# A graph-attention and GraphSAGE kernel: the first batch prepared in halves by a written order, block 0's signs read by two engines, the output bias added in parts

## The chip, the cores and the metric

The kernel runs on one core of one Trainium2 chip. The core has TensorE (PE in the profile, PEld for its weight loads), VectorE (DVE), ScalarE (ACT), GpSimd (POOL) and SyncE (SP). SP issues most DMAs; POOL issues some through the software queue. The metric is the device time of a launch in microseconds: the median of the runs, with a profiled execution beside it.

## The reference, cut to what matters

There are 16 batches of 1024 nodes with 128 features. `x` is [16, 1024, 128] in float32, `adj` is a sparse weighted adjacency [16, 1024, 1024] in float32, and `nodemask` is all ones here.

```python
# layer 0: attention
h = relu(layernorm(x))
q, k, v = (h @ W.T + b for each)                 # 8 heads of 16
scores = where(adj == 0, -inf, q k^T / 4)
attn = softmax(scores) * adj
attn = attn / (attn.sum(-1) + 1e-8)
x = x + (attn @ v) @ Wo.T + bo

# layer 1: dilation of the neighbourhoods, then three SAGE layers
h = relu(layernorm(x))
adj_d = adj * keep      # row by row: rank of each neighbour, every sf-th of more than 10 removed,
                        # symmetrically; earlier rows' removals count for later rows
for i in 1..3:
    agg = adj_d @ h / clip(sum(adj_d), 1)
    out = agg @ Wr_i + h @ Wx_i + b_i
    h = batchnorm(relu(out / |out| * mask))      # statistics over all batches and nodes
    h_i = h
x = x + (concat(h_1, h_2, h_3) * mask @ Wl + bl) * mask
```

## The kernel before, in words

The work is one long program in two parts. The order of the instructions of PE, ACT and DVE in the main part is the order in which Python writes them (`manual_schedule`, line 1087). SP's and POOL's instructions, and everything in front of that line, `first_part`'s set-up among it, stand in the order that a scheduler chose.

**Part one** is attention with the dilation beside it. `attention` (line 403) runs over 256 turns (batch b, half c of the query nodes, block m of 128 key nodes), and each turn has two half-turns g, one for each group of four heads. A half-turn on PE adds the mask to the scores (`never` times `nomask`, line 488), adds the products of `qT` and `kT` (line 494), and sums the values of the half-turn before (lines 410 and 415). ACT takes the exponential (two instructions at line 510), and DVE multiplies by the adjacency (two at line 515). So the pair of exponentials marks a half-turn: the text numbers them half-turn 0, 1, 2 and so on. `turn_over` (line 433) prepares a turn two turns ahead: a block of the adjacency is transposed on PE, copied by ACT (line 444), stored to `aT_d`, turned into `nomask` (line 448), and six small DMAs shift `nomask` between partitions (lines 452 and 453). `load` (line 423) brings the block in, three tiles ahead, on SP.

`prepare` (line 254) makes what attention needs of one batch: layer norm (`layer_norm_relu`, line 231; statistics on DVE, the power -1/2 on POOL at line 244, the scaling on ACT at line 250), the transposed activations `hT`, and from them `kT`, `v1` and `qT`. It is a generator, and every `yield` names the place at which the next step may be put. For the batches 1 to 15 its steps are strewn over the half-turns of the batch before. For batch 0 nothing runs yet: lines 461 to 465 turn over two turns and then run all the steps of `prepare(0)` in one go, up to `ready[0]`, before the first score.

`dilation` (line 549) works on 8 blocks of 128 rows of all 16 batches, and `beside_attention` (line 825) puts its steps between the half-turns, paced by the count of half-turns, never by a clock. At its start it reads block 0 of every batch: `fetch(0, b)` (line 573) loads 128 rows by 1024 columns in float32 (512 KB) from `adj` on SP into a tile `ad` with two buffers, and `read(0, b)` (line 579) makes its signs with two ACT instructions that also count the edges. Two batches are read in each of the half-turns 0 to 7. Behind this block the rows of the next blocks are read between other work.

**Part two** is the three SAGE layers L = 0, 1, 2, each with 32 turns (b, c). PE sums over the neighbours (`pg`, line 1011), and for the turn before it DVE and ACT form `o` (line 1029), its squares (line 1034), the square root of their sum (line 1040), the scaled result (line 1044), and PE transposes it (line 1048). In between DVE masks the adjacency of the turn to come (line 139, four pieces). In layer 1, each turn with c = 0 ends with `add_bias` (line 913): ACT multiplies the output bias by the mask of each of the 8 node blocks into `tb`, and DVE adds `tb` to `prev`, the running output.

The tag names the buffer: `mr` has four of 4 KB per partition, which the dilation's working tiles use in part one; `ad` has two; `ps_m` and `ps_d` are PSUM pools of one bank each. `biases` (lines 87 to 100 here, without a function) splits five bias vectors into three bfloat16 pieces, whose rows PE adds by a matmul with ones.

Of the kernel before, what the change touches and what calls it, by code (L numbers as in the profile page):

```python
# [10 lines left out]
F32 = mybir.dt.float32  # L11
BF = mybir.dt.bfloat16
# [9 lines left out]
P = 128  # L22
# [12 lines left out]
def swept(ctx: ExitStack, tc: tile.TileContext, t: dict, out: bass.AP, flag: bass.AP):  # L35
# [52 lines left out]
    n = len(names)  # L88
    bias3 = const.tile([3, n, D], BF, name="bias3")
    with tc.tile_pool(name="setup", bufs=1) as where:  # L90
        vecs = where.tile([1, 2, n, D], F32, name="vecs")
        for i, name in enumerate(names):
            nc.sync.dma_start(vecs[:, 0, i, :], t[name].rearrange("(o d) -> o d", o=1))
        pieces = where.tile([1, 3, n, D], BF, name="pieces")
        for i in range(3):
            nc.vector.tensor_copy(pieces[:, i], vecs[:, i % 2])
            if i < 2:
                nc.vector.tensor_tensor(vecs[:, 1 - i], vecs[:, i], pieces[:, i], ALU.subtract)
        for i in range(3):
            nc.sync.dma_start(bias3[i : i + 1], pieces[:, i])  # L100
# [60 lines left out]
    def first_part(p1):  # L161
# [7 lines left out]
        def load_x(b):  # L169
            if b < B:  # L170
                xts[b] = shared.tile([P, NB, D], F32, name=f"xt_{b}", tag="xin", bufs=3)
                nc.sync.dma_start(xts[b], x[b].rearrange("(k p) d -> p k d", p=P))

        load_x(0)


        nr_i = pool.tile([B * NB, P], I32, name="nr_i", tag="qT")
        nc.sync.dma_start(nr_i, nodemask.rearrange("b (k p) -> (b k) p", p=P))
        nr_f = pool.tile([B * NB, P], F32, name="nr_f", tag="qT")
        nc.vector.tensor_copy(nr_f, nr_i)  # L180
        mps = ps_m.tile([P, 512], F32, name="mps", tag="m")
        nc.tensor.transpose(mps[:, : B * NB], nr_f, ident[: B * NB, : B * NB])
        nc.vector.tensor_copy(mf, mps[:, : B * NB])
        nc.vector.tensor_tensor(mf2, mf, mf, ALU.mult)
        nc.vector.tensor_scalar(
            kill.rearrange("p b k -> p (b k)"), mf, 0.0, -1e5, ALU.is_equal, ALU.mult
        )
# [6 lines left out]
        wps = ps_m.tile([P, 4, D], F32, name="wps", tag="m")  # L194
        for i in range(4):
            nc.tensor.transpose(wps[:, i, :], raw[:, i, :], ident)
        attn_w = one.tile([P, 4, D], F32, name="attn_w")
        nc.vector.tensor_copy(attn_w, wps)
# [13 lines left out]
        nc.vector.tensor_tensor(bq[:, 0:2], own, bq[:, 2:3].to_broadcast([P, 2]), ALU.mult)  # L212
# [3 lines left out]
        for v1 in v1s:  # L216
            nc.gpsimd.memset(v1, 0.0)
            nc.gpsimd.memset(v1[:, :, :, HD : HD + 1], 1.0)
# [5 lines left out]
        zeros = one.tile([P, B * 2 * NB], F32, name="zeros")  # L224
        eps8 = one.tile([P, 32], F32, name="eps8")
# [5 lines left out]
        def layer_norm_relu(dst, src, name):  # L231

            st = shared.tile([P, NB, 6], F32, name=f"st_{name}", tag="lnst", bufs=2)
            mv = shared.tile([P, NB, 2], F32, name=f"mv_{name}", tag="lnmv", bufs=2)
            for i in range(0, NB, 2):
# [4 lines left out]
                if i + 2 < NB:  # L240
                    yield False
            rs = shared.tile([P, 2, NB], F32, name=f"rs_{name}", tag="lnrs", bufs=2)
            nc.vector.tensor_scalar(rs[:, 1, :], mv[:, :, 1], LN_EPS, None, ALU.add)
            nc.gpsimd.tensor_tensor(rs[:, 0, :], rs[:, 1, :], minus_half, ALU.pow)
            yield False
            nc.vector.scalar_tensor_tensor(rs[:, 1, :], mv[:, :, 0], -1.0, rs[:, 0, :], ALU.mult, ALU.mult)
            for i in range(0, NB, 2):
# [6 lines left out]
        def prepare(b):  # L254
# [5 lines left out]
            yield from layer_norm_relu(h, xt, f"a{b}")  # L260
            hT = shared.tile([P, N], F32, name=f"hT_{b}", tag="s", bufs=2)
            for c in range(2):
                yield True
                pt = ps_m.tile([P, 512], F32, name=f"pt_{b}_{c}", tag="m")
# [4 lines left out]

            kT = pool.tile([P, N], F32, name=f"kT_{b}", tag="kT")  # L270
            def query(c):
                pq = ps_m.tile([P, 512], F32, name=f"pq_{b}_{c}", tag="m")
# [7 lines left out]
            def key(c):  # L280
                cc = slice(c * HN, (c + 1) * HN)
                pk = ps_m.tile([P, 512], F32, name=f"pk_{b}_{c}", tag="m")
# [6 lines left out]
            def value(c):  # L289
                pv = ps_m.tile([P, HB, D], F32, name=f"pv_{b}_{c}", tag="m")  # L290
# [11 lines left out]
            for what in (key, value):  # L302
                yield True
                yield from what(0)

            yield "half 1"
            qTs = [pool.tile([P, 2, HN], F32, name=f"qT_{b}_0", tag="qT")]
            yield True
            yield from query(0)
# [93 lines left out]
        def attention():  # L403
# [16 lines left out]
            turns = [(b, c, m) for b in range(B) for c in range(2) for m in range(NB)]  # L420
            tiles = {}

            def load(i):
                if i >= len(turns):
                    return
                b, c, m = turns[i]
                a = pool.tile([P, HB, P], F32, name=f"a_{b}_{c}_{m}", tag="a", bufs=3)
                nc.sync.dma_start(
# [1364 lines left out]
```

## Time and profile before

| | |
|---|---|
| median of 3 runs | 3615.09 us (3610.25 to 3615.42) |
| the profiled execution | 3607.07 us, span 3605.3 us |
| busy in the span | PE 95%, DVE 88%, ACT 64%, POOL 5% |
| first exponential of attention | 36.14 us |
| half-turns 0 to 7, from there to 94.97 us | 58.8 us |
| the 14 half-turns from 95.0 to 153.9 us | 58.9 us |
| layer 1, one turn with c = 0 and the next with c = 1 | 10.48 and 12.71 us |
| layer 2, the same two | 10.47 and 11.67 us |

A profile shows one execution, in microseconds from the span's start. A busy engine need not be the bound; what counts is what ended each wait, and which engine waits for it. A window row gives, for one stretch of time, the busy time and the count of instructions of PE, PEld, DVE, ACT and POOL, the TensorE clock that was granted, the busy share of the DMA engines and their rate. A timeline row gives the start, the duration, the engine, the line, the operation, the tiles, and in brackets how long the engine had been idle and what ended it. SPq is SP's queue of DMA issues: its duration is that of the issue, not of the transfer.

### The profile page before, as it was taken

The page shows a single profiled execution, that of the slowest core. Times are in us where ns is not written, and L with a number is a line of the kernel's source. Part 1 is how long each engine was busy: PE and PEld are TensorE (multiplying, and loading weights), DVE is VectorE, ACT ScalarE, POOL GpSimd, SP SyncE. Part 2 cuts the span into 40 slices and gives each one's busy share as a digit, 9 for nine tenths or more (in the row PEclk, how much of TensorE's full clock was granted, in tenths as well). Part 3 has the DMA queues.
Part 4 walks back from the last instruction along what each step waited for, and adds up shares of the span by engine and source line. Part 5 has one row for each costly group of instructions (what it writes and reads, how often), then busy time and mean ns, then how long its engine had stood idle before and what let it go on. Part 6 is the DMA issues. An engine that isn't in the chain of part 4 may idle for free.

```text
span 3605.3 us, 86057 instructions
## 1 busy us (share of the span) xinstructions
PE 3437.5 (95%) x34855; PEld 1889.5 (52%) x34855; DVE 3159.5 (88%) x5215; ACT 2300.5 (64%) x3813; POOL 168.2 (5%) x232
## 2 busy tenths in 40 slices
PE   6999999999999999999999999999999899999997
PEld 2333333333333333333333333337999898989996
DVE  3899999889989999999999999997778788878886
ACT  5689779769859968967876986873222333322224
POOL 1000000000000000000000000000000000000000
PEclk9999999999999999999999999999999999999999
DMA  5346447537636736744853773677999789889995
GB/s 183 116 137 201 144 123 208 162 114 205 197 111 193 222 107 178 230 137 142 234 177 118 234 219 108 189 226 272 327 329 331 247 319 321 322 295 333 334 332 195
DMA packets 651011, 772.79 MB, mean 214 GB/s; under 512 B 173125, under 2 KB 570058, under 8 KB 638314
## 3 DMA queue, kind: packets, MB, share of 16 engines
q1 hardware_dynamic: 637706, 718.29, 61.9%
q0 software_dynamic: 12896, 48.90, 3.9%
q8 instruction: 275, 4.51, 0.5%
q14 instruction: 134, 1.10, 0.1%
HBM read 509.02 MB, written 157.29 MB: 185 GB/s over the span
## 4 chain that ended last, share of the span: by engine, by line
PE 44%; DVE 41%; ACT 6%; DMA 5%; issue 3%; SPq 2%; ACTq 0%; POOL 0%; DVEq 0%; POOLq 0%
DVE w L515 15%; PE pg L1011 14%; PE sc L494 6%; PE acc L410 5%; PE acc L415 4%; DVE wr L782 4%; DVE hit L717 3%; DVE aT L139 3%; ACT e L510 3%; PE pn L982 2%; PE sc L488 2%; PE own L997 2%; DMA nomask<-nomask 2%; PE pt L1048 2%; DVE o L1029 1%
## 5 line engine op out<-in xcount | busy, mean ns | idle before, releaser
L515 DVE TENSOR_TENSOR w<-e,aT 128x1024 f32<-128x1024 f32 x1024 | 1203.7, 1216 | 155.1 <-ACT e L510 154.6
L510 ACT ACTIVATE e<-sc 128x1024 f32<-128x1024 f32 x1024 | 990.5, 1020 | 405.3 <-PE sc L494 404.1
L1011 PE MATMUL pg<-y,aT 128*128 128x128 f32 (+1 forms) x6144 | 739.2, 275 | 0.0
L1011 PEld LDWEIGHTS pg<-y,aT 128*128 128x128 f32 x6144 | 713.4, 192 | 0.0
L410 PE MATMUL acc<-w,v_both 128*32 128x512 f32 x4096 | 647.2, 614 | 6.4 <-DVE w L515 2.7
L415 PE MATMUL acc<-e,eps 128*32 128x512 f32 x4096 | 621.3, 596 | 0.0
L494 PE MATMUL sc<-qT,kT 32*128 32x512 f32 x4096 | 592.2, 648 | 0.3 <-ACT qT L276 0.3
L139 DVE SCALAR_TENSOR_TENSOR aT<-mr,aT 128x1024 f32<-128x1024 bf16 x384 | 458.6, 1216 | 0.0
L415 PEld LDWEIGHTS acc<-e,eps 128*32 128x32 f32 x4096 | 157.9, 111 | 303.7 <-issue 295.5
L1034 ACT ACTIVATE sq<-o 128x512 f32<-128x512 f32 x96 | 60.6, 631 | 362.6 <-DVE o L1029 362.6
L782 DVE TENSOR_TENSOR_SCAN wr<-rk 128x1024 f16<-128x1024 bf16 x128 | 291.6, 2278 | 0.0
L488 PE MATMUL sc<-nomask,never 32*32 32x512 bf16 x8192 | 247.5, 387 | 27.0 <-ACT e L510 20.8
L488 PEld LDWEIGHTS <-never 32*32 32x32 bf16 x8192 | 78.3, 88 | 311.8 <-issue 290.1
L494 PEld LDWEIGHTS sc<-qT,kT 32*128 32x128 f32 x4096 | 161.5, 184 | 118.1 <-issue 117.3
L441 PEld LDWEIGHTS pa<-ident,a 128*128 128x128 f32 x1024 | 109.9, 143 | 199.0 <-issue 150.6
L410 PEld LDWEIGHTS acc<-w,v_both 128*32 128x32 f32 x4096 | 100.2, 108 | 210.5 <-DVE w L515 110.0
L1049 ACT COPY hT<-pt 128x512 f32<-128x512 f32 x96 | 56.2, 585 | 236.0 <-PE pt L1048 236.0
L795 ACT ACTIVATE wr<-wr,th 128x1024 f16<-128x1024 f16 x128 | 147.9, 1156 | 46.6 <-DVE wr L782 45.7
L441 PE MATMUL pa<-ident,a 128*128 128x128 f32 x1024 | 171.9, 292 | 2.2 <-DMA a<-in_adj 1.5
L448 ACT ACTIVATE nomask<-aT 128x512 bf16<-128x512 f32 x256 | 161.4, 630 | 8.2
L1029 DVE SCALAR_TENSOR_TENSOR o<-pg,rdeg,mine 128x128 f32<-128x128 f32 x384 | 108.0, 344 | 61.2 <-PE pg L1011 59.8
L444 ACT COPY aT<-pa 128x512 f32<-128x512 f32 x256 | 151.5, 592 | 9.6 <-PE pa L441 9.6
(214 smaller groups left out, 3930.4 us busy)
## 6 DMA issues: line engine op xcount, KB each, us to landing
aT<-aT_d SPq DMA_DIRECT2D x94, 2048.0 KB, 9.7
mr<-mr_d SPq DMA_DIRECT2D x188, 512.0 KB, 6.0
a<-in_adj SPq DMA_DIRECT2D x256, 256.0 KB, 4.0
aT_d<-aT SPq DMA_DIRECT2D x256, 256.0 KB, 4.1
ad<-in_adj SPq DMA_DIRECT2D x128, 512.0 KB, 4.3
nomask<-nomask SPq DMA_DIRECT2D x512, 96.0 KB, 2.3
nomask<-nomask SPq DMA_DIRECT2D x512, 64.0 KB, 2.6
nomask<-nomask SPq DMA_DIRECT2D x512, 32.0 KB, 2.5
```

The costliest lines, as they stand in the source:

```text
L139: nc.vector.scalar_tensor_tensor(part, mrs[h][:, j : j + 2, :].rearrange("p j n -> p (j n)"), 0.0, part, ALU.is_equal, ALU.mult)
L410: nc.tensor.matmul(acc[g][32 * j : 32 * j + 32, :], v1[:, m, 2 * j + g, :], ws[j // 2][:, j % 2, :], start=(m == 0), stop=False,)
L415: nc.tensor.matmul(acc[g][32 * j : 32 * j + 32, :], eps8, es[j // 2][:, j % 2, :], start=False, stop=(m == NB - 1),)
L441: nc.tensor.transpose(pa[:, k * P : (k + 1) * P], a[:, k, :], ident)
L444: nc.scalar.copy(aT[:, 0, :], pa)
L448: nc.scalar.activation(nomask[:, 0, :], aT[:, 0, :], AF.Relu, bias=1.0, scale=-1e38, accum_out=zeros[:, i : i + 1])
L488: nc.tensor.matmul(scs[j // 2][to : to + 32, j % 2, :], never[rows, rows], nomask[rows, j, :], start=True, stop=False, tile_position=(32 * ...
L494: nc.tensor.matmul(scs[j // 2][:, j % 2, :], kT[rows, mm], qTs[c][rows, g, :], start=False, stop=True, tile_position=(32 * j, 0),)
L510: nc.scalar.activation(e, scs[q], AF.Exp, scale=1.0 / math.sqrt(HD))
L515: nc.vector.tensor_tensor(w, es[q], aT.to_broadcast([P, 2, HN]), ALU.mult)
L782: nc.vector.tensor_tensor_scan(wrs[b], rk(b, 1, N + 1), rk(b, 2, N + 2), -1023.0, ALU.add, ALU.add)
L1011: nc.tensor.matmul(pg[:, i // 2, at : at + width], aT[:, j, i * P : (i + 1) * P], y[:, j, :width], start=(j == 0), stop=(j == NB - 1),)
```

## The change

Batch 0 is prepared in two halves of its nodes. `layer_norm_relu` takes a range, and `prepare(0)` has a branch of its own that yields names at which the caller does other first work: the transposed weights (`turn_weights`), the bias pieces (`biases`), the second turn's adjacency (`first_turns[1]`). Attention may start when the first half has its `hT`, `kT` and `qT` and the second half is normalised; `value(0)`, `turned(1)`, `key(1)`, `value(1)` follow beside the first half-turns. `first_part` is called inside `manual_schedule`, so PE, ACT and DVE keep the written order there too. `node_masks` moves into half-turn 0. The first three adjacency blocks are issued by ACT, x of batch 0 is SP's first DMA, and the bias vectors go through POOL. `v1`'s upper half is cleared by DVE instead of all of it by POOL. A batch of `x` is not loaded again when it is there already.

Block 0 of the dilation is fetched through POOL's queue into the four `mr` buffers, four batches ahead. The odd batches' signs are made on DVE.

`add_bias` becomes a generator: four multiplications after the first quarter of the turn's sums, four after the second, and DVE's addition where it was.

```diff
+    def biases():
+        vecs = [shared.tile([1, n, D], F32, name=f"vecs{i}", tag="mr", bufs=4) for i in range(2)]
         for i, name in enumerate(names):
-            nc.sync.dma_start(vecs[:, 0, i, :], ...)
+            nc.gpsimd.dma_start(vecs[0][:, i, :], ...)
+        yield
...
-            nc.sync.dma_start(bias3[i : i + 1], pieces[:, i])
+            nc.gpsimd.dma_start(bias3[i : i + 1], pieces[:, i])
+        yield
...
         load_x(0)
+        for i in range(3):
+            load(i, nc.scalar)
+        bias_pieces = biases()
+        next(bias_pieces)
...
+        def turn_weights():
+            wps = ps_d.tile([P, 4, D], F32, name="wps", tag="d")
+            for i in range(4):
+                nc.tensor.transpose(wps[:, i, :], raw[:, i, :], ident)
+            yield
+            nc.vector.tensor_copy(attn_w, wps)
+            nc.vector.tensor_tensor(bq[:, 0:2], own, bq[:, 2:3].to_broadcast([P, 2]), ALU.mult)
+            yield
...
         for v1 in v1s:
-            nc.gpsimd.memset(v1, 0.0)
-            nc.gpsimd.memset(v1[:, :, :, HD : HD + 1], 1.0)
+            nc.vector.memset(v1[:, :, :, HD:], 0.0)
+            nc.vector.memset(v1[:, :, :, HD : HD + 1], 1.0)
...
+            if b == 0:
+                first = layer_norm_relu(h, xt, "a0", 0, HB)
+                for _ in range(2):
+                    next(first)
+                yield "weights"
+                yield from first
+                yield "weights"
+                yield "biases"
+                yield from turned(0)
+                yield "turn 1"
+                second = layer_norm_relu(h, xt, "a0", HB, NB)
+                for _ in range(2):
+                    next(second)
+                yield from key(0)
+                qTs = [pool.tile([P, 2, HN], F32, name=f"qT_{b}_0", tag="qT")]
+                yield from query(0, (ps_d, "d"))
+                yield from second
+                ready[b] = (xt, qTs, kT, v1)
+                yield True
+                yield from value(0, (ps_d, "d"))
+                yield True
+                yield from turned(1)
...
-            for i in range(2):
-                for _ in turn_over(i):
-                    pass
-            take_on(prepare(0), 0)
-            while 0 not in ready:
-                go_on_with(True, False, "evict", "first", "half 1")
+            first_turns = [turn_over(i) for i in range(2)]
+            weights = turn_weights()
+            next(first_turns[0])
+            next(first_turns[0], None)
+            rest = prepare(0)
+            for step in rest:
+                if step == "weights":
+                    next(weights)
+                elif step == "turn 1":
+                    for _ in first_turns[1]:
+                        pass
+                elif step == "biases":
+                    next(bias_pieces)
+                elif 0 in ready:
+                    beside.append([rest, step])
+                    break
...
             def fetch(k, b):
+                if k == 0:
+                    blocks[0][2][b] = shared.tile([P, N], F32, name=f"ad_0_{b}", tag="mr", bufs=4)
+                    nc.gpsimd.dma_start(blocks[0][2][b], adj[b, :P, :])
+                    return
...
             def read(k, b):
+                if k == 0 and b % 2:
+                    for part, of, count in (
+                        (rk(b, 2, 2 + n1), ad[:, :n1], signs[:, k, 0, b : b + 1]),
+                        (rk(b, 2 + n1, N + 2), ad[:, n1:], blocks[k][1][:, b : b + 1]),
+                    ):
+                        nc.vector.scalar_tensor_tensor(
+                            part, of, 0.0, nothing.to_broadcast([P, of.shape[-1]]), ALU.add, ALU.not_equal,
+                            accum_out=count,
+                        )
+                    return
...
+            for b in range(4):
+                fetch(0, b)
             for b in range(B):
-                fetch(0, b)
                 read(0, b)
+                if b + 4 < B:
+                    fetch(0, b + 4)
                 yield 0.3, b % 2
...
     def add_bias(b, prev):
-        for k in range(NB):
-            nc.scalar.mul(tb[:, k, :], wts["bl"], mf[:, b * NB + k : b * NB + k + 1])
+        for k0 in (0, HB):
+            for k in range(k0, k0 + HB):
+                nc.scalar.mul(tb[:, k, :], wts["bl"], mf[:, b * NB + k : b * NB + k + 1])
+            yield
         nc.vector.tensor_tensor(prev, prev, tb, ALU.add)
+        yield
...
+                    if biased:
+                        next(biased)
                     pieces[0]()
                     if before:
                         go(before, "norm")
...
+                    if biased:
+                        next(biased)
                     if before:
                         go(before, "transposed")
...
-                    if c == 0 and L == 1:
-                        add_bias(b, prev)
+                    if biased:
+                        next(biased)
                     go(this, "sums")
```

## The prediction

> **What bounds the kernel now.** I read the page first, then three stretches of the window view, then the timeline of each engine where a stretch stood out.
>
> ```profile
> span 3605.3 us, 86057 instructions
> ...
> PE   6999999999999999999999999999999899999997
> DVE  3899999889989999999999999997778788878886
> ```
>
> PE is over 90% busy in nearly every slice (90 us each), except the first; DVE is next. So there is little to win in the middle, and the first slice is the place to look. The window view divides it (time, span of the window, then busy us and counts of PE, PEld, DVE, ACT, POOL, the granted clock, DMA share, GB/s):
>
> ```profile
> 0.00:36.10 36.10, 15.91 (x59) 7.38 (x60) 8.23 (x40) 10.86 (x21) 12.29 (x25) 1.00 0.58 169
> 36.10:95.00 58.90, 43.13 (x354) 13.67 (x354) 21.60 (x35) 43.77 (x101) 1.64 (x1) 0.91 0.60 192
> 95.00:180.00 85.00, 81.00 (x931) 28.50 (x930) 79.64 (x113) 53.26 (x79) 0.39 (x2) 0.94 0.37 112
> 300.00:600.00 300.00, 293.58 (x3263) 106.83 (x3262) 282.74 (x429) 250.51 (x404) 14.11 (x14) 0.99 0.55 161
> ```
>
> Up to 36.1 us, the first exponential, the busiest engine, PE, works 44% of the time: it is a chain. From 36.1 to 95 DVE stands at 37%, against 94% later, and DMA moves only 192 GB/s. Eight half-turns take 58.8 us there (exponentials at 36.14 and 94.97), and 14 take the 58.9 us that follow. The timelines name the wait:
>
> ```profile
> 14.81 0.49 DVE L237 BATCH_NORM_STATS2 st_a<-xt 128x6 f32<-128x128 f32 x2 [5.47 <-DMA xt<-in_x]
> ...
> 36.14 1.94 ACT L510 ACTIVATE e<-sc 128x1024 f32<-128x1024 f32 x2 [1.51 <-PE sc L494]
> ...
> 57.78 0.31 ACT L582 ACTIVATE rk<-ad 128x128 bf16<-128x128 f32 x1 [2.73 <-DMA ad<-in_adj]
> ...
> 91.70 0.31 ACT L582 ACTIVATE rk<-ad 128x128 bf16<-128x128 f32 x1 [4.70 <-DMA ad<-in_adj]
> ```
> ```profile
> 58.53 6.95 SPq L576 DMA_DIRECT2D ad<-in_adj  x4
> 65.57 0.39 SPq L428 DMA_DIRECT2D a<-in_adj  x1
> ```
>
> Batch 0 waits until 14.8 for its x, which SP issues behind 18 other DMAs. After 36 ACT waits for `ad` (14.9 us in five waits), and the exponentials queue behind it. Two `ad` buffers make SP hold its queue for seven microseconds in every turn, with the next `a`, its store and the `nomask` shifts behind it; so the wait is one of buffers and queue order, not of bandwidth. The third place is layer 1:
>
> ```profile
> 3009.48 1.22 DVE L919 TENSOR_TENSOR acc<-acc,tb 128x1024 f32<-128x1024 f32 x1 [3.57 <-ACT tb L918]
> ...
> 3015.86 0.66 PE L1048 MATMUL pt<-ident,o 128*128 128x128 f32 x4 [0.83 <-DVE o L1044]
> ```
> ```profile
> 3319.32 0.60 PE L1048 MATMUL pt<-ident,o 128*128 128x128 f32 x4
> ```
>
> DVE stands 3.57 us for the eight bias products, so `o` of that turn starts at 10.62 instead of at 8.2, when PE's sums end; the c = 1 turn's transposes then wait 0.83 us, which layer 2 does not have.
>
> **What the Trainium skill says.** "DMA: Bandwidth & Descriptors", section "Queues, rings and completion order": each DMA engine takes turns between the queues that have work, by packets, and consumes one ring in order. So POOL's `ad` tiles take a share from SP's backlog while both have work; the trace of before has no such overlap here. Same page, "Where 436 GB/s comes from": about 358 GB/s from HBM for a core. The trace agrees in kind: its best slices are at 334. "SBUF — State Buffer", section "Who interferes with whom": a DMA issued by POOL can starve while DVE runs a mode that takes both ports. In this trace POOL's 512 KB loads land in 7.0 us (`h0in`, median), SP's `ad` in 4.3: slower, whatever the cause. "TensorE: Matmul & The Clock Gate", Part 1: after some idle microseconds the array runs at half clock until it is busy again. The trace agrees: eight `sc` matmuls take 2.09 us at 34 us and 1.14 us at 45.5.
>
> **Part A, up to the first exponential.** x becomes SP's first issue, at about 0.74 (when the first is now). The three `a` blocks go out beside it on ACT: 0.52 + 0.79 MB at the 276 GB/s of the 10 to 20 us window is 4.8 us; with 2 us for a first landing (0.74 to 3.3 in the trace for the vectors), x is there at 7.5. Two pairs of statistics and the addition take 1.4 (rows at 14.8 to 17.4): 8.9. The power waits for POOL, which has ahead of it five bias DMAs and six norm DMAs of 0.6, the masks 1.5 and the two small memsets 0.3: 8.4 from 0.7, so 9.1; with 1.67 for the power and 0.17 for DVE, 10.9. Four scalings at 0.40, transposes, `hT` 0.6: 13.5. Turn 1's transposes 1.1, `kT`'s matmul 2.1, `qT`'s 2.1, its evictions 1.5, all at the cold durations of before: about 19.7. Meanwhile DVE does weights 0.9, pieces 3.2 (rows L96, L98), statistics 1.4 to 16.4, POOL's second power ends at 18.1, and the four scalings run behind `qT` to 21.3. Scores 2.1 behind `qT`: 21.8. So 22 is the early end, 14 us ahead.
>
> The late end is `nomask` of turn 0. SP issues x of the batches 1 and 2, two `ad` of block 1 and `a` of turn 3 ahead of it: with x, the weights and the `a` blocks 4.6 MB, 16.7 us at 276 GB/s, so 19 alone. From 13 us POOL's first `ad` tiles (2.1 MB) take up to half: up to 7 us more, scores behind: 28. I take 25: **11 us** (8 to 14). DVE's clearing of `v1` (four memsets, some 2.4 us at one element per cycle as in L66) lies before x lands and is free; without that cover it adds to the chain.
>
> **Part B, half-turns 0 to 7.** ACT loses 8 of 16 sign pairs (1.32 each with their reads) and DVE gets them: 1.08 for 896 columns and 0.28 for 128 (the like instructions at L599) plus two 0.08 reads, about 1.45. DVE then has 2.3 + 0.75 + 1.45 = 4.5 per half-turn, ACT 1.8 + 1.3 + 1.3 = 4.4, PE 4 to 4.5: a pace of 4.8, with 5.5 for the first two at cold clock: 40. The node masks (1.0 on DVE) lie in the wait for the first exponential. DMA: up to the last sign x 1.6, weights 0.3, eight `a` 2.1, 18 `ad` 9.4, six stores 1.6, six sets of shifts 2.4: 17.4 MB, of which 6.2 are through by 25. The other 11.2 MB at the 300 of the best longer stretches are 37; the last exponential follows 2 to 3 us behind: 65 to 67 as well. So 42 instead of 58.8: **17 us**. Bounds: 36 at the later pace (23 won), 50 at 250 GB/s (9 won). A second load of batch 2's x (17 `xt` loads in the page, for 16 batches) goes away: 0.5 MB, in the sum above. SP's 16 moved `ad` issues no longer stand before `a`, stores and shifts; in POOL's queue only batch 1's power stands between them, with half a turn to spare.
>
> From half-turn 8 the instructions stand as before, and the dilation is paced by count, so A and B carry to the end unchanged.
>
> **Part C, the bias.** The c = 1 turn takes 12.71 us in layer 1 and 11.67 in layer 2; with the products done early, DVE's sum fits in the 3.57 us gap behind the statistics, and 1.04 us go, 16 times: 16.6. Against it: the first four products (1.2 us) stand on ACT ahead of the square root of the turn before. It would end 1.2 later, of which DVE's mask piece hides 0.9; the reciprocal, `o` and PE's transposes come 0.3 late: 15 times, 4.8. The second four end before `hT` is due. **11 us** (0 if the delay doubles and half of the gain shows; 16 if it is hidden). `prev` lands in time: its load is issued a turn before (3008.95, landing 9.7 later, for an addition at about 3029).
>
> **Sum.** 11 + 17 + 11 = 39. On the profiled execution's 3607.07 us (its span 3605.3) that gives 3568. The median of the runs lies 8 above it, and I take 39 from it: **3576 us**.
>
> **Rivals.**
> 1. DMA is the next bound (25 of 100): software-queue tiles land late, the eight half-turns take 50 or more and `nomask` is late: A 8, B 7, C 11: 3589. For it: 17.4 MB in 65 us is close to the best rate, and POOL's loads are slower. Against: rows of 4 KB, and four tiles in flight.
> 2. The bias gives nothing (12): the root's delay costs what the early sum wins: 28, 3587. Against it stands layer 2's turn, where DVE waits 2.4 us for PE.
> 3. All goes well (10): 14 + 23 + 14: 3564.
> 4. Slower (5): each half-turn waits for a tile asked for two half-turns earlier. To use up A and C too, the eight half-turns must take 81 us, 10.1 each, so a tile must need some 20 us to land; at 22 us the time is 8 x 11 = 88, 29 lost against 22 won: 3622. POOL's 512 KB landed within 12.5 us at worst, under a fuller DMA load.
> 5. It comes back (3): later waits take up the early start; no change, 3612. No wait after 95 us is tied to a clock, so only steered work could do it, and there is none.
>
> The forecast has 45. A measurement of this kernel can tell about 0.2%, 7 us, from no change: faster 0.92, same 0.03, slower 0.05. The range is 3560 (all goes well, less the runs' 5 us spread) to 3600 (a half of B and none of C).
>
> **What would show it.** A: first exponential near 25; at 28 or more with its scores behind a `nomask` DMA, the queue was the cause. B: half-turn 8 near 67, DVE over 80% busy from 30 to 65, DMA near 300; waits of ACT or DVE for `ad` would speak for rival 1. C: no wait of DVE for `tb`, layer 1's c = 1 turn at 11.7, its c = 0 turn at 10.8. Wrong altogether if half-turns past the eighth are slower than 4.2 to 4.5 us, or a tile on POOL's queue needs more than 10 us.

## The result, and the profile after

The kernel after takes 3573.93 us (median of four runs, 3571.68 to 3574.51), beside 3613.14 us before (3610.25 to 3615.42): a ratio of 0.989, with a 95% interval of 0.9877 to 0.9901. The forecast was 3576. The profiled execution took 3571.68 us, beside 3607.07 before; the spans differ by 35.4 us, the medians by 39.2.

The page of the kernel after, its span and the busy tenths in 40 slices (90 us each):

```profile
span 3569.9 us, 86070 instructions
...
PE   8999999999999999999999999999999899999997
...
DVE  7999999989989999999999999987778788878886
```

PE's first digit goes from 6 to 8 and DVE's from 3 to 7; otherwise three of DVE's digits move by one. The windows of the kernel after (time, length, busy us and counts of PE, PEld, DVE, ACT and POOL, granted clock, DMA share, GB/s):

```profile
0.00:24.00 24.00, 11.49 (x33) 4.66 (x34) 9.91 (x44) 9.80 (x19) 13.34 (x32) 0.98 0.90 269
24.00:64.00 40.00, 39.11 (x362) 14.30 (x361) 30.48 (x66) 33.64 (x68) 10.97 (x15) 0.89 0.87 281
64.00:149.00 85.00, 81.64 (x949) 29.16 (x947) 80.22 (x117) 53.90 (x81) 0.40 (x2) 0.98 0.34 102
```

Before, PE was busy 43 us of the 59 that half-turns 0 to 7 took, and DMA moved 192 GB/s. Now PE is busy 39.1 of 40 us and DMA moves 281 GB/s. In the kernel after, DVE waits 3.8 us for tiles `ad` in these half-turns and ACT 0.5, where ACT waited 14.9 before.

The timeline of the kernel after up to its first exponential (start, duration, engine, line, tiles; in brackets the idle time and what ended it), and the exponential of half-turn 8:

```profile
20.90 0.39 PE L540 MATMUL sc<-nomask,never 32*32 32x512 bf16 x3 [0.86 <-DMA nomask<-nomask]
...
24.51 0.61 PE L540 MATMUL sc<-nomask,never 32*32 32x512 bf16 x3 [0.58 <-DMA nomask<-nomask]
25.05 2.09 PE L546 MATMUL sc<-qT,kT 32*128 32x512 f32 x8
...
27.17 1.94 ACT L565 ACTIVATE e<-sc 128x1024 f32<-128x1024 f32 x2 [4.45 <-PE sc L546]
...
64.86 1.94 ACT L565 ACTIVATE e<-sc 128x1024 f32<-128x1024 f32 x2
```

Half-turn 8 in the kernel before:

```profile
94.97 1.91 ACT L510 ACTIVATE e<-sc 128x1024 f32<-128x1024 f32 x2
```

The score matmuls stand behind the shifts of `nomask`. ACT had its second half of `h` done at 22.7, so 4.45 us go there. From half-turn 8 to half-turn 22, 14 half-turns take 62.0 us (64.86 to 126.86), 4.4 each; before they took 63.0 (94.97 to 157.94), 4.5 each, and not the 58.9 of the table ahead, which counts the exponentials that start in that stretch.

In layer 1 (line 995 is DVE's addition of the bias, line 1125 PE's transposes, once in each turn):

```profile
2945.83 0.18 DVE L1119 RECIPROCAL f<-f 128x4 f32<-128x4 f32 x1 [0.15 <-ACT f L1117]
2947.07 0.63 PE L1125 MATMUL pt<-ident,o 128*128 128x128 f32 x4 [0.64 <-DVE o L1121]
2949.72 1.21 DVE L995 TENSOR_TENSOR acc<-acc,tb 128x1024 f32<-128x1024 f32 x1
2958.77 0.60 PE L1125 MATMUL pt<-ident,o 128*128 128x128 f32 x4
2969.46 0.63 PE L1125 MATMUL pt<-ident,o 128*128 128x128 f32 x4 [0.64 <-DVE o L1121]
```

DVE's wait of 3.57 us for `tb` (at 3009.48 before) is gone, and with it PE's 0.83 in one turn. The other turn pays: the reciprocal waits 0.15 for ACT's root, and the transposes wait 0.64, where in the kernel before they waited 0.41:

```profile
3003.17 0.63 PE L1048 MATMUL pt<-ident,o 128*128 128x128 f32 x4 [0.41 <-DVE o L1044]
```

From one row of line 1125 to the next are 11.70 and 10.69 us in the kernel after.

How far the kernel after is ahead of the kernel before, along the program (a root is one row of the square root, one in each turn of part two):

| | before | after | ahead |
|---|---|---|---|
| first exponential | 36.14 | 27.17 | 9.0 |
| half-turn 8 | 94.97 | 64.86 | 30.1 |
| half-turn 60 | 331.22 | 302.37 | 28.9 |
| first root of layer 0 | 2478.93 | 2451.70 | 27.2 |
| last root of layer 0 | 2799.94 | 2772.80 | 27.1 |
| last root of layer 1 | 3182.61 | 3142.53 | 40.1 |
| first root of layer 2 | 3205.32 | 3168.04 | 37.3 |
| last root of layer 2 | 3545.05 | 3507.81 | 37.2 |
| end of the span | 3605.3 | 3569.9 | 35.4 |

So 30 us come in the first 65, 13 in layer 1, and about 8 are given back elsewhere: 3 inside attention, 2.8 between layers 1 and 2, and 1.8 at the end. A second profile of the same kernel (near the end of the next section) does not give back the first two.

### The profile page after: what moved, and what is told of

Same layout as the page of the kernel before. It is cut to its first block, busy times and chain, and to the rows that moved or that the text cites. A ratio compares the mean times of both kernels' runs of the same rounds, so it can differ in the third digit from the quotient of the medians.

```text
span 3569.9 us, 86070 instructions
## 1 busy us (share of the span) xinstructions
PE 3437.5 (96%) x34855; PEld 1893.6 (53%) x34855; DVE 3175.4 (89%) x5254; ACT 2290.3 (64%) x3781; POOL 179.0 (5%) x253
## 4 chain that ended last, share of the span: by engine, by line
PE 50%; DVE 37%; ACT 6%; DMA 4%; issue 2%; SPq 1%; ACTq 0%; POOL 0%; DVEq 0%
PE pg L1088 16%; DVE w L570 15%; PE sc L546 7%; PE acc L467 6%; PE acc L472 5%; DVE wr L855 4%; DVE hit L790 3%; PE pn L1059 2%; PE sc L540 2%; ACT e L565 2%; PE own L1074 2%; PE py L1003 2%; PE pt L1125 1%; PE pa L485 1%; DMA nomask<-nomask 1%
```

## The experiments

The experiments are edits of the kernel after. They ran on several chips, on each beside runs of the kernel before (medians 3614 to 3617), so times are compared as ratios to those, and stages as rows of one profile each. The kernel after has the ratio 0.9889 (0.9877 to 0.9901). Of the intervals below, only that of the first experiment lies clear of it; what the others show is read from the stages.

How far two profiles differ where the instructions are the same has to be known first. Four profiles have the kernel after's instructions up to half-turn 8: its own two, and those of the two bias versions below. Their first exponential came at 27.17, 26.05, 28.32 and 28.10, their half-turn 8 at 64.86, 62.14, 64.42 and 64.62. So a difference below 3 us between two profiles there shows nothing.

### Half-turns 0 to 7, piece by piece

Three things changed for block 0's tiles: four buffers for two, POOL's queue for SP's, and DVE making half of the signs. First all three were put back.

```diff
-                if k == 0:
-                    blocks[0][2][b] = shared.tile([P, N], F32, name=f"ad_0_{b}", tag="mr", bufs=4)
-                    nc.gpsimd.dma_start(blocks[0][2][b], adj[b, :P, :])
-                    return
...
-                if k == 0 and b % 2:
+                if False:
...
-            for b in range(4):
-                fetch(0, b)
             for b in range(B):
+                fetch(0, b)
                 read(0, b)
-                if b + 4 < B:
-                    fetch(0, b + 4)
```

> The kernel after, with block 0 of the dilation read as before: on SP's queue, two buffers of tag ad, all signs on ACT. Theory (part B is the block's own buffers, queue and shared signs): the first exponential stays at 27.2 and half-turn 8 comes 55 to 59 us behind it, at 82 to 86 instead of 64.9; the time 18 to 21 higher, 3592 to 3595. Rival (the half-turns became fast because batch 0's other work, the second x load and the node masks went out of their way): half-turn 8 at 65 to 72, the time 3574 to 3581.

The ratio is 0.9923 (0.9907 to 0.994). By the medians' ratios that is some 12 us above the kernel after, less than the 18 to 21 of the theory, but the spans of the two profiles differ by 18.9 (3588.8 and 3569.9). The profile has half-turn 8 at 83.64, where the theory had it. But the first exponential did not stay. The timeline of this version:

```profile
21.61 1.14 PE L546 MATMUL sc<-qT,kT 32*128 32x512 f32 x8
...
22.78 1.94 ACT L565 ACTIVATE e<-sc 128x1024 f32<-128x1024 f32 x2
...
36.70 0.31 ACT L647 ACTIVATE rk<-ad 128x128 bf16<-128x128 f32 x1 [4.81 <-DMA ad<-in_adj]
...
83.64 1.91 ACT L565 ACTIVATE e<-sc 128x1024 f32<-128x1024 f32 x2
```

It comes at 22.78, without a wait for `nomask`, and the scores run at 1.14 us for eight where the kernel after has 2.09. Then ACT waits for `ad` again. So at half-turn 8 part A is worth 94.97 - 83.64 = 11.3 us, and part B 83.64 - 64.86 = 18.8. Part B takes back 4.4 at the first exponential. With half-turn 8 of the kernel after anywhere from 62.1 to 64.9, part B is worth 18.8 to 21.5.

One piece at a time. All signs on ACT, with POOL's queue and four buffers (`if k == 0 and b % 2:` becomes `if False:`):

> The kernel after, with POOL's queue and the four buffers kept, but all signs of block 0 on ACT. If ACT's own work then sets the pace (my theory: exponentials 1.9, two pairs of signs 2 x 1.5 and a turn's copies 0.9, about 5.8 us in each half-turn), half-turn 8 comes 46 us behind the first exponential, at 73, and the time is 8 higher, 3582. If the buffers and the queue alone made part B (rival 1), half-turn 8 stays at 65 to 67 and the time within 2 us of 3574. If the sharing alone made it (rival 2), it goes to 82 to 86 and 3592 to 3595, as with the signs all as before.

Half-turn 8 came at 72.83, 45.3 us behind a first exponential at 27.57, and the ratio is 0.990 (0.9883 to 0.9916). The window of this version:

```profile
24.00:64.00 40.00, 33.54 (x317) 12.17 (x315) 19.49 (x36) 35.08 (x80) 8.13 (x14) 0.93 0.82 257
```

ACT is busy 35.1 of 40 us, PE 33.5 and DVE 19.5. My theory met the pace, 45.3 us for 46, and both rivals fell: without the sharing ACT is the busiest engine and the half-turns are longer.

SP's queue and two buffers as before, with the signs shared:

> The kernel after, with block 0 read through SP and two `ad` buffers as before, but the odd batches' signs on DVE. The kernel with all of it as before had its first exponential at 22.8 and half-turn 8 at 83.6, 7.6 us for a half-turn. Theory (the period is one of buffers: a tile is asked for when its buffer has been read, and the next signs wait for its landing; about 2.8 of reading in a row on one engine and 4.3 to land): reading by two engines side by side takes 1.4 off, 6.0 to 6.2 each, half-turn 8 at 71 to 73. Rival (SP's other issues set the period): 80 to 84, as without the sharing. Second rival (sharing is what part B is): 60 to 65.

Half-turn 8 at 78.31, 55.9 us behind the first exponential at 22.37, between the theory's 71 to 73 and the first rival's 80 to 84; ratio 0.9923 (0.9898 to 0.9948). In this version's list of waits (engine and line, what it waited for: us in total, times, longest), over half-turns 0 to 7:

```profile
DVE rk L642 <- DMA ad<-in_adj: 22.6, 7, 5.0
ACT rk L647 <- DMA ad<-in_adj: 20.6, 6, 6.2
```

and in its timeline SP's issue of four tiles, seven microseconds as before:

```profile
31.22 7.03 SPq L631 DMA_DIRECT2D ad<-in_adj  x4
```

With two buffers both engines wait. Reading a pair in parallel takes 0.6 us off a half-turn (7.6 to 7.0), not the 1.4 of the theory. A tile lands 4.4 us after its issue (median), and the second of a pair waits in SP's queue; that this is why the gain was small is my reading, not shown.

POOL's queue and shared signs, with two buffers (`tag="ad", bufs=2`, and two tiles fetched ahead):

> The kernel after (POOL's queue, shared signs) with two `ad` buffers for block 0 instead of four. Theory (the four buffers carry part B): a tile on POOL's queue needs 6.7 us to land and about 1 to be issued, so with two buffers a half-turn takes 1.4 + 6.7 + 0.5 to 1, 8.6 to 9.1; half-turn 8 some 70 us behind the first exponential, which comes at 23 to 25 since fewer tiles compete with the shifts of nomask: half-turn 8 at 92 to 97, slower than with everything as before (83.6). Rival (taking the tiles out of SP's queue carries it): half-turn 8 at 64 to 70.

Half-turn 8 at 74.71, 52.7 us behind the first exponential at 21.98; ratio 0.9903 (0.9878 to 0.9928). Neither figure was met. The landing times of `ad`, in this version:

```profile
DMA to landing us min/median/max: 3.8/4.8/6.3
```

and in the kernel after:

```profile
DMA to landing us min/median/max: 4.0/6.7/7.8
```

I had taken 6.7 us for the price of POOL's queue. It is not: with two buffers the same queue lands a tile in 4.8. The two missing buffers still cost 9.8 us at half-turn 8.

Four buffers and shared signs, issued by SP (`nc.gpsimd.dma_start` becomes `nc.sync.dma_start`):

> The kernel after with the four buffers and the shared signs, the tiles issued by SP instead of POOL. Theory (buffers and sharing make part B, the queue adds little): half-turns of 4.6 to 5, half-turn 8 about 37 to 40 us behind the first exponential, which comes at 27 to 30 because four more tiles stand ahead of the shifts of nomask: 65 to 70, the time 3574 to 3580. Rival (SP's queue is the point: it stands at a fetch until a buffer is read, with the next block, its store and the shifts behind it): half-turns of 6 and more, half-turn 8 past 77, the time 3586 or more.

Half-turn 8 at 65.89, ratio 0.988 (0.9855 to 0.9906): 1.0 us behind the kernel after's first profile, which is within the difference between profiles. The theory held on where it ends, and missed how. The first exponential came at 22.69, not late, because these tiles now stand behind the shifts of `nomask`, and the half-turns took 43.2 us instead of 37.7 (36.1 to 37.7 in the four profiles). The waits of this version in that stretch:

```profile
DVE rk L647 <- DMA ad<-in_adj: 9.8, 4, 4.2
ACT rk L652 <- DMA ad<-in_adj: 7.6, 4, 3.9
```

From half-turn 2 on SP issues the tiles four at a time, every second half-turn. So POOL's queue wins 5.5 us in the half-turns and loses 4.5 ahead of them.

| block 0's tiles | first exponential | half-turn 8 |
|---|---|---|
| SP, 2 buffers, ACT | 22.78 | 83.64 |
| SP, 2 buffers, both engines | 22.37 | 78.31 |
| POOL, 2 buffers, both | 21.98 | 74.71 |
| SP, 4 buffers, both | 22.69 | 65.89 |
| POOL, 4 buffers, ACT | 27.57 | 72.83 |
| POOL, 4 buffers, both (the kernel after) | 27.17 | 64.86 |

The buffers are worth 12.4 us on SP and 9.8 on POOL, the sharing 5.3 with two buffers and 8.0 with four, the queue 3.6 with two buffers and 1.0 with four. Each is the difference of two profiles, so the worth of buffers and sharing is clear, that of the queue is not.

### Is bandwidth the next bound?

The first rival of the prediction. The tiles of block 0 were cut to half their bytes:

```diff
-                    nc.gpsimd.dma_start(blocks[0][2][b], adj[b, :P, :])
+                    nc.gpsimd.dma_start(blocks[0][2][b][:, :HN], adj[b, :P, :HN])
...
+                    ad = ad[:, :HN].unsqueeze(1).to_broadcast([P, 2, HN])
+                        (rk(b, 2, 2 + n1), ad[:, 0, :n1], ...),
+                        (rk(b, 2 + n1, N + 2)..., ad[:, :, HN - 448 :], ...),
```

> The kernel after, loading only the first 512 of the 1024 columns of block 0's tiles (4.2 MB less on the way to half-turn 8 of the 17.7 MB that move); the signs of the columns 64 to 511 are written in place of the others', so the later dilation works on other signs, with the same instructions. Theory (the pace behind the first exponential is set by the engines, PE busy 39.1 of 40 us): half-turn 8 comes 36 to 38 behind the first exponential as in the kernel after (37.7); the first exponential itself comes at 22.5 to 25. Rival (bandwidth sets it, 17.7 MB at 270 to 280 GB/s being 64.9 us): 13.5 MB are 49 us, so half-turn 8 at 50 to 56, 28 to 33 behind the first exponential.

Half-turn 8 came at 63.19, 37.2 us behind the first exponential at 25.97. (With these signs the program goes on, behind its end, into a second program for uncommon inputs, `walked`, so its 13013 us in all say nothing.) The window of this version:

```profile
24.00:64.00 40.00, 39.62 (x375) 14.36 (x375) 31.67 (x70) 35.20 (x71) 10.91 (x15) 0.88 0.62 186
```

The rate fell from 281 to 186 GB/s, no engine waits for `ad` any more, and the stretch is as long as it was (36.1 to 37.7 us): bandwidth is not the bound there. The busiest engine is PE, with 39.6 of 40 us, but no run takes work from PE, and ACT is close: from 35 to 64 us it is busy 28.1 of 29 us in the kernel after. So that the bytes do not set the pace is shown, and that PE does is only likely. The first exponential gained little with half of POOL's bytes.

### The first exponential

```diff
+            held = [shared.tile([P, N], F32, name=f"held{i}", tag="ad", bufs=2) for i in range(2)]
...
                 read(0, b)
+                if b == 9:
+                    for h in held:
+                        nc.vector.memset(h[:, :1], 0.0)
...
-            load_x(2)
...
+                    if i == 0 and g == 1:
+                        load_x(2, nc.scalar)
```

> The kernel after, with two SP loads of the dilation's block 1 (1 MB) held back until block 0's tenth tile is read, and x of batch 2 (0.5 MB) loaded on ACT's queue in half-turn 1. Theory (the first exponential came at 27.2 instead of 22.8 because the shifts of nomask stand behind these loads in SP's queue and share the bandwidth with them): the first exponential at 23 to 24, the time 3 to 4 lower, 3570. Rival (the shifts are late by themselves, from POOL's block 0 tiles that move at the same time): the first exponential at 26 to 27, no change. Where the two loads are then missed later, half-turns 8 to 12 would be slower.

Its timeline has the first exponential with no wait in front of it:

```profile
22.71 1.92 ACT L564 ACTIVATE e<-sc 128x1024 f32<-128x1024 f32 x2
```

4.5 us earlier than in the kernel after (3.3 to 5.6 earlier than in the four profiles), and half-turn 8 comes at 60.86, 1.3 to 4.0 earlier. The ratio is 0.9869 (0.9849 to 0.9888). So taking SP's three early loads away is enough, and so is taking POOL's four tiles away (the first experiment): `nomask` is late only when both are there. The other versions agree: the five further profiles with both (the kernel after again, all signs on ACT, the halved tiles, the two bias versions) have it at 26.0 to 28.3, and the five others without one of the two at 20.6 to 22.7.

### The bias

The whole of `add_bias` put back at the end of the c = 0 turn:

```diff
-                    if biased:
-                        next(biased)
                     pieces[0]()
...
-                    if biased:
-                        next(biased)
                     if before:
                         go(before, "transposed")
...
                     if biased:
-                        next(biased)
+                        whole(biased)
```

> The kernel after, with all eight bias products put back at the end of the c = 0 turn. Theory (part C is worth what the turns show: 1.04 us won in each of 16 c = 1 turns, 0.25 lost in each c = 0 turn, 12.4 in all): layer 1 back to 10.47 and 12.71 us, the time 12 above the kernel after's 3574: 3586. Rival (part C's gain was an accident of where the turns stood, and is taken up elsewhere, since the end of layer 2 lost 2.3 against before): 3574 to 3577. The first 2400 us of the span stand as in the kernel after for both.

Measured: 3585.42 us, ratio 0.991 (0.9893 to 0.9926), span 3583.0. PE's transposes in its layer 1:

```profile
2945.11 0.66 PE L1125 MATMUL pt<-ident,o 128*128 128x128 f32 x4 [0.83 <-DVE o L1121]
2955.62 0.63 PE L1125 MATMUL pt<-ident,o 128*128 128x128 f32 x4 [0.40 <-DVE o L1121]
2968.31 0.66 PE L1125 MATMUL pt<-ident,o 128*128 128x128 f32 x4 [0.83 <-DVE o L1121]
```

A pair of turns takes 23.20 us, against 22.39 in the kernel after: 0.81 x 16 = 13 us in layer 1. The theory held in the turns. In the time, the two intervals overlap. Next, the first four products behind the root, the second four behind the transposes:

```diff
-                    if biased:
-                        next(biased)
                     pieces[0]()
                     if before:
                         go(before, "norm")
+                    if biased:
+                        next(biased)
...
-                    if biased:
-                        next(biased)
                     if before:
                         go(before, "transposed")
+                    if biased:
+                        next(biased)
```

> The kernel after with the first four bias products put behind the square root of the turn before, and the second four behind its transposes. Theory (the c = 0 turn of layer 1 grew by 0.25 because four products stood ahead of the root): c = 0 back to 10.47, c = 1 still 11.67; 3.7 lower than the kernel after's time. Rival (the eight products are ACT time that the turn has not got in any place, or the second four now come too late for DVE's addition): the c = 0 turn stays at 10.7 or the c = 1 turn goes to 12: no gain, or up to 5 slower.

The same rows of this version:

```profile
2948.03 0.63 PE L1125 MATMUL pt<-ident,o 128*128 128x128 f32 x4 [0.40 <-DVE o L1121]
2959.72 0.60 PE L1125 MATMUL pt<-ident,o 128*128 128x128 f32 x4
2970.17 0.63 PE L1125 MATMUL pt<-ident,o 128*128 128x128 f32 x4 [0.40 <-DVE o L1121]
```

The pair takes 22.14, as in layer 2. From the first to the last root layer 1 takes 340.3 us instead of 343.7. The place of the products was what the c = 0 turn paid for. The time does not show it: 3573.55 us (0.9893, 0.9876 to 0.991) beside 3569.70 of the kernel after on the same chip; 3.4 us is below what these runs can tell.

### The kernel after again, and the repairs together

> The kernel after once more, beside the two versions below on one chip, so that they have it to be compared with: 0.989 of the kernel before; half-turn 8 at 64.9 within 0.5, layer 1's turns at 10.72 and 11.67. What differs from the first profile of it (inside attention, and in the first matmuls of a layer) is the variation from run to run.

The ratio is 0.9884 (0.9866 to 0.9902), 3569.70 us. The first exponential came at 26.05 and half-turn 8 at 62.14, so one profile is good to about 3 us there, more than the 0.5 that I had written. Its span of 3561.2 us is 44.1 below that of the kernel before, where the first profile had 35.4, and the medians differ by 44.5. It is 32.8 us ahead at half-turn 8, 33.8 at the last root of layer 0, and 46.3 at the last root of layer 1 and at both roots of layer 2: nothing comes back in attention or between the layers. Layer 1 took 343.6 us from first to last root, as before. The gap from layer 1's last root to layer 2's first was 22.7 us here and 25.5 in the first profile. The first matmuls of layer 2, in the kernel after:

```profile
3149.52 2.07 PE L1059 MATMUL pn<-weights,h 128*128 128x128 f32 x8 [1.01 <-ACT h L1052]
3152.27 2.08 PE L1059 MATMUL pn<-weights,h 128*128 128x128 f32 x8 [0.68 <-ACT y L1061]
```

and in the same kernel again:

```profile
3143.29 1.16 PE L1059 MATMUL pn<-weights,h 128*128 128x128 f32 x8 [1.79 <-ACT h L1052]
3145.13 1.16 PE L1059 MATMUL pn<-weights,h 128*128 128x128 f32 x8 [0.68 <-ACT y L1061]
```

The same instructions take 2.07 or 1.16 us. The granted clock was 0.50 in the one stretch (3149.5 to 3154.5) and 1.00 in the other (3143.2 to 3148.0).

All three repairs were then put together; the one that is new holds back the six norm vectors' DMAs, which stood ahead of the first power on POOL, by a `memset` of their tile on DVE at `read(0, 9)`.

> The kernel after with all three repairs: the two loads of block 1 and batch 2's x held back, the six norm vectors' DMAs on POOL held back as well so that they do not stand ahead of the first power -1/2, and the bias products behind the square root. Theory: the power starts at 7.9 instead of 10.0, the first exponential at 20.5 to 21.5 (22.7 without the last point), half-turn 8 at 58.5 to 61; layer 1 3.7 less; in all 8 to 10 lower than the kernel after's time. Rival (what is won at the first exponential is taken by waits for `ad` before half-turn 8, as these tiles now come too late): half-turn 8 at 61 as with the loads alone, 7 to 8 lower.

The first exponential came at 20.57, as the theory had it, and half-turn 8 at 62.00, 1.0 behind the rival's 61. The power ran at 7.96 instead of 10.03. The ratio is 0.9876 (0.9859 to 0.9892), beside 0.9884. POOL's timeline in this version:

```profile
46.09 0.53 POOL L634 DMA_DIRECT2D ad<-in_adj  x1 [1.47 <-DVE norms L689]
46.60 0.54 POOL L1160 DMA_DIRECT2D norms<-in_L_gnn_g  x1
...
50.03 0.53 POOL L1161 DMA_DIRECT2D norms<-in_L_gnn_be  x1 [0.78 <-DMA ad<-in_adj]
52.65 0.53 POOL L634 DMA_DIRECT2D ad<-in_adj  x1 [2.08 <-ACT nomask L492]
```

and the waits of ACT and DVE at the last two of block 0's tiles:

```profile
59.99 0.31 ACT L653 ACTIVATE rk<-ad 128x128 bf16<-128x128 f32 x1 [3.32 <-DMA ad<-in_adj]
...
61.86 0.29 DVE L648 SCALAR_TENSOR_TENSOR rk<-ad,nothing 128x128 bf16<-128x128 f32 x1 [4.75 <-DMA ad<-in_adj]
```

The DMAs that were moved came to stand ahead of block 0's last two fetches, and ACT's wait stands ahead of the exponential of half-turn 8. So they were moved once more, behind the last tile:

```diff
+                if b == B - 1:
+                    nc.vector.memset(norms, 0.0)
                 yield 0.3, b % 2
```

> As the version with all three repairs, but the six norm vectors' DMAs are held back until block 0's last tile has been read, so that on POOL they stand behind the last two tile fetches and not ahead of them (there they kept these fetches from about 49 to 53 us, and half-turn 8 came at 62.0). Theory: the first exponential at 20.6 as there, half-turn 8 at 58.5 to 60 with no wait for `ad` above 2 us behind half-turn 6, layer 1 as there, 3.3 shorter than in the kernel after: 8 lower than it, 0.986 of the kernel before. Rival (block 0's tiles need what they need in bytes and landings, whatever stands ahead of them): half-turn 8 still at 61 to 62, 5 to 6 lower, 0.987.

The longest wait for `ad` behind half-turn 6 fell to 1.5 us; half-turn 8 came at 60.71 behind a first exponential at 21.47, between the theory's 58.5 to 60 and the rival's 61 to 62. The time is 3566.91 us, 0.9862 (0.9845 to 0.9878) of the kernel before: the lowest ratio of all, but its interval meets those of the kernel after (0.9889 and 0.9884), so it is not shown to be faster than it.

## Why the prediction was right, step by step

The forecast of 3576 stands 2 us above the median, and the three places and their mechanisms were right. In the prediction's own terms part A is the first exponential, part B the length of half-turns 0 to 7: 11, 17 and 11 were predicted, 9.0, 21.2 and 13 measured in the first profile. A too large and B too small cancel in part. (With part B undone, A alone was worth 11.3 at half-turn 8, and B the other 18.8.) The sum of the three in the first profile, 43, is above the 39.2 by which the medians differ; in the second set of runs the medians differ by 44.5. So the change is worth 39 to 45 us, and that the forecast stands within 2 us is in part luck.

- **Part A, the chain.** `qT` was put at 19.7 with its evictions done; they start at 19.75 and end at 21.20. The terms that the prediction lists behind its 13.5 add up to 20.3 already. On the way x landed at 6.4, not 7.5, and POOL took up the power at 10.03, not 9.1, as two of the norm DMAs ahead of it waited 0.44 and 1.17 us for bias vectors to land. The early end of 22 is nearly what the versions without a late `nomask` and with the power at 10.0 to 10.3 have (22.4 to 22.8), but by luck: `qT` was some 1.5 late, and the eight score matmuls took 1.14 there, not 2.1.
- **Part A, the late end.** The mechanism was right: `nomask` behind SP's loads, with POOL's tiles beside them. I took 25 between 22 and 28; it was 27.2 and 26.1, and 28.3 and 28.1 in the bias versions. The term that was mis-sized is the share that POOL's tiles take: up to 7 us, of which I took about half. Against the 22.8 without them it is 3.3 to 5.5 us. A microsecond of it is clock: the eight score matmuls took 2.09 us behind those waits, with a granted clock of 0.50 (25.0 to 27.2), and 1.14 where there was none, with 1.00 (21.6 to 22.8 in the first experiment). In the kernel before, the clock column reads 1.00 where they take 2.09, so there only the durations show the lower rate.
- **Part B, the pace.** I had 5.5 for each of the first two half-turns and 4.8 for the others; measured are 10.7 for the two and 4.5 for the others, 37.7 us in all instead of 40. I then took 42, because the bytes gave the same end. The bytes were right (17.8 MB in the first 66 us, 17.4 predicted), but the step from them to a bound failed: with 186 GB/s instead of 281 the stretch was as long. In the kernel after, ACT and DVE waited 4.3 us for tiles, and POOL's next fetches 25 us for ACT and DVE to be done with a buffer: the tiles waited for the engines. DVE was busy 83% from 30 to 65 (29.0 of 35 us), as predicted.
- **POOL's queue.** The prediction feared tiles at 10 to 20 us; the slowest took 7.8. "SBUF — State Buffer", section "Who interferes with whom", of the Trainium skill says that a DMA issued by POOL can starve while DVE runs a mode that takes both ports. With DVE busy 83% and tiles landing in 6.7, or in 4.8 with fewer in flight, no run here shows it; whether DVE ran such a mode in that stretch is not known.
- **From half-turn 8 on.** "Carry to the end unchanged" held to about 3 us (30.1 and 27.1), and to 1 in the second profile (32.8 and 33.8). That is the difference between profiles: from half-turn 60 to the first root of layer 0 the runs of versions with the same instructions there take 2147 to 2156 us.
- **Part C.** The turns came as predicted: 11.67 and 10.8 were written, 11.70 and 10.69 measured. The price of 0.3 in the c = 0 turn was 0.23 (the transposes' wait, 0.64 for 0.41), and it had the cause that was named, the root behind four products: with the products moved behind it the wait is 0.40.
- **The rivals.** Bandwidth as next bound fell with the halved tiles. A bias without gain fell with the bias undone. The slower case fell with the landing times. "It comes back" fell: what the first profile loses between layers, 2.8 us, is the clock and is not lost in the second, and the 1.8 at the end lies within what the versions with the same instructions there differ by (60.4 to 62.4 us behind the last root, 60.2 in the kernel before).

Open is why PE stays at the lower rate between layers 1 and 2. The gap is 25.5 to 25.7 us in ten of the twelve profiles with the bias in parts, and 22.7 in the other two, in the kernel before and in the version with the bias undone. That is a leaning, no proof, and no run tells apart whether the change brings it on.

## What to carry to other kernels

A stall that looks like a slow DMA can be one of buffers: at the same queue, four tiles instead of two were worth 10 to 12 us here, and the queue alone 1 to 4, where profiles of one kernel differ by 3. A transfer moved out of the way stands in the way of something else, so list what is behind it on its new queue: the six norm DMAs held up the power by 2 us where they were, and at the next place ACT and DVE waited 3.3 and 4.8 us for the tiles behind them. When a byte count and an engine count give the same end, only halving one of them tells which binds. And before a difference of two profiles is read, a second profile of the same kernel tells how much of it is scatter.

## What was not expected of the hardware

The landing time of a 512 KB tile on POOL's queue went with what was in flight, 4.8 us with two buffers and 6.7 with four, and was mostly no price of the queue: SP's were 4.4 and 5.9. With four tiles of 256 KB in flight it was 3.9, so the bytes matter and not the number alone. Eight matmuls at the head of a layer took 1.16 us in one run and 2.07 in another of one kernel, at a granted clock of 1.00 and 0.50, and the gap between the layers moved by 2.8 us with it.
